# Order in the first attention of an adaptive block: queries scaled by ScalarE, transposes ahead of maxima, gathers behind divisions, merges ahead of the last product

## The chip, the cores and the metric

The kernel runs on one core of a Trainium2 chip. Its engines are named as in the profile: PE (TensorE, matmuls; PEld is its loading of weights), DVE (VectorE), ACT (ScalarE), POOL (GpSimd) and SP (SyncE, which issues most of the transfers). The metric is the time on the device in microseconds (us), as a median of several runs. The time before is 1429.85 us (three runs, 1428.89 to 1431.21).

## The reference

The block computes, on `x` of 8 batches of 128 tokens by 512 values:

```python
x = x + attn(cond(x, weight, adapter_ids), wq, wk, wv, wo)
x = x + ffn(cond2(x, ...))

def cond(x, weight, adapter_ids):          # a 512x512 matrix per batch
    return jnp.einsum('bsi,boi->bso', x, weight[adapter_ids])

def attn(x, wq, wk, wv, wo):               # 32 heads of 16, 8 pairs of keys and values
    q = (x @ wq).reshape(b, s, 32, 16)
    k = jnp.repeat((x @ wk).reshape(b, s, 8, 16), 4, axis=2)
    v = jnp.repeat((x @ wv).reshape(b, s, 8, 16), 4, axis=2)
    scores = jnp.einsum('bihd,bjhd->bhij', q, k) * 16 ** -0.5
    scores = jnp.where(causal, scores, finfo.min)
    out = jnp.einsum('bhij,bjhd->bihd', softmax(scores), v)
    return out.reshape(b, s, 512) @ wo
...
```

`cond2` is a second attention, with 32 heads of 128, rotary positions, and a cache of keys and values of which pages are looked up in a table. `ffn` is a matrix product with low-rank matrices added, one pair chosen for each batch and one shared. All numbers are float32.

## The kernel before

The kernel has two parts that share the core one after the other: the first attention (with the conditioning matrix), up to about 224 us, and the second attention with the feed-forward, which takes the rest. Both are written as explicit sequences: a manual schedule keeps every engine's instructions in the order in which the Python code issues them. The framework adds the semaphores: an instruction waits until what it reads is written and until the buffer that it writes is free, and what stands behind it on the same engine waits too.

The first attention is a loop over `k` from 0 to 16 (L719). Each batch `b` has two steps, an even one (`hb == 0`, k = 2b) and an odd one (k = 2b + 1), and each step handles half of the batch's heads. Within a step the probabilities lie in two tiles, `n` = 0 and 1.

- `scores1(k)` (L586): TensorE writes the causal mask (L595) and adds the products of scaled queries and keys (L607) in two PSUM tiles of 128x1024. At its end VectorE takes the negated row maxima of both tiles (L616).
- `exps1(k, n)` (L628): ScalarE, eight exponentials for each tile (L635), which read the scores and the maxima.
- `divide1(k, n)` (L639): VectorE sums and inverts (L643, L644), then GpSimd multiplies the 128x1024 tile by the inverses (L645).
- `turn1(k)` (L649): VectorE transposes both tiles of a step in blocks of 32x32 (L655). It is issued for the step before, `last`, directly behind the scores and maxima of the step at hand.
- `values1(b, groups)` (L659): TensorE multiplies the transposed probabilities by the values (L671), and VectorE copies the result (`oT`, L683). It is issued in the even step for the batch before, in two halves.
- `condition(b)` (L507): TensorE multiplies the transposed input by the gathered matrix (`hp`, L514), and VectorE copies it out (`hT`, L522; by ScalarE for batch 0). In the even step, for the next batch; then its keys (`project_k`, L545) and values (`project_v`, L552) are projected from `hT`.
- `project_q(b, ...)` (L530) and `keep_q(b)` (L538): in the odd step, the queries of the next batch, 16 matmuls (32 rows of the trace), and VectorE's scaling of the 128x512 tile into `qT` (L540). Behind it `flip_x` (L502) transposes a later batch's input, which ScalarE copies (L505).
- `out_proj1(b)` (L690): in the odd step, the output product (L693), the residual addition by VectorE (L697) and a store. `flip_x1` (L700) transposes the sum in the next even step, with a copy by ScalarE (L702).
- `gather_w(b)` (L293): GpSimd issues four indirect transfers (L296) of the conditioning matrix of a batch. It is called at the end of the even step, for batch b + 3.
- `indices()` (L374): VectorE works out the addresses for the cached pages (L377 to L382), in the odd step of batch 0. They are first read by `gather(0, ...)`, in the odd step of batch 6. `tables(0)` and `tables(1)` are GpSimd work (L414 to L416) in the odd steps of batches 1 and 2.
- `merge_gates` (L441, L447, VectorE, at the end of step 12), `merge_a` (L457, step 14), `merge_b` (L469) and `merge_w` (L484) prepare the low-rank matrices of the feed-forward. `merge_b(h)` is eight rows of TensorE in the trace, a copy by ScalarE (L477) and a store; `merge_w(i)` two, with an addition by VectorE (L491).

In the last step (k = 16) only the values product of batch 7 is left. Before it, in step 15, the first unit of the second attention is projected (`q_matmul`, `q_turn`, `kv_matmul`, `kv_turn`, `norms`). Step 16 issues, in this order: both transposes, `flip_x1(6)`, `queries(0)` (transposes of the first unit's queries, L254), the first half of `values1(7)`, `merge_b(0)`, its second half, `merge_b(1)`, `merge_w(0)` and `merge_w(1)`. Behind the loop come `keys(0)` (L263), `own_keys(0)` (L271) and the other two `merge_w`.

PSUM tiles that matter: `p_mm` (tag `mm`, two buffers) holds the projections, the output product and the merges; `p_tp` (two buffers) the flips and the values product; `p_sc` (two buffers) the scores.

Of the kernel before, what the change touches and what calls it, by code (L numbers as in the profile page):

```python
# [14 lines left out]
AF = mybir.ActivationFunctionType  # L15
ALU = mybir.AluOpType
# [4 lines left out]
B, S, DM = 8, 128, 512  # L21
# [8 lines left out]
SCALE1 = HD1 ** -0.5  # L30
# [11 lines left out]
def block_kernel(  # L42
# [28 lines left out]
    nc = tc.nc  # L71
# [178 lines left out]
    def queries(u):  # L250
        s = st[u]
        tp = p_tp.tile([P, REP, S], F32, tag="tp", name=f"qTp_{u}")
        for r in range(REP):
            nc.tensor.transpose(tp[:, r, :], s["qa"][:, r, :], ident[:])  # L254
        s["qT"] = tile_a([P, REP, S], f"qT_{u}")
        nc.scalar.copy(s["qT"][:], tp[:])  # L256
# [19 lines left out]
    with (  # L276
# [216 lines left out]
        xT, hT, qT, kbd = {}, {}, {}, {}  # L493
# [43 lines left out]

        def keep_q(b, ps):  # L538
            qT[b] = p1.tile([P, REP, S], F32, tag="qT1", name=f"qT1_{b}")
            nc.vector.tensor_scalar(qT[b][:], ps[:], SCALE1, None, ALU.mult)  # L540

        def project_k(b):
            ps = p_mm.tile([P, 2, P], F32, tag="mm", name=f"kvp1_{b}")
# [40 lines left out]
        H = [{} for _ in range(2 * B)]  # L584

        def scores1(k):  # L586
            b, hb = divmod(k, 2)
            h = H[k]
            h["sc"] = [
                p_sc.tile([P, 2, 4 * S], F32, tag="sc", name=f"sc1_{k}_{n}") for n in range(2)  # L590
            ]
            for c in range(4):
                for j in range(4):
                    rows = slice(32 * j, 32 * j + 32)
                    nc.tensor.matmul(  # L595
                        h["sc"][j // 2][:, j % 2, :].rearrange("p (n t) -> p n t", n=4)[
                            :, :, 32 * c : 32 * c + 32
                        ],
                        causal[rows, c, :],
                        eye32[rows],  # L600
                        start=(c == 0),
                        stop=False,
                    )
            for rr in range(2):
                for j in range(4):
                    rows = slice(32 * j, 32 * j + 32)
                    nc.tensor.matmul(  # L607
                        h["sc"][j // 2][:, j % 2, rr * 2 * S : (rr + 1) * 2 * S],
                        qT[b][rows, 2 * hb + rr, :],
                        kbd[b][rows].rearrange("p h t -> p (h t)"),  # L610
                        start=False,
                        stop=(rr == 1),
                    )
            h["nm"] = p1.tile([P, 2, 8], F32, tag="nm1", name=f"nm1_{k}")
            for n in range(2):
                nc.vector.tensor_reduce(  # L616
                    h["nm"][:, n, :],
                    h["sc"][n][:].rearrange("p j (h t) -> p (j h) t", t=S),
                    AX.X,
                    ALU.max,  # L620
                    negate=True,
                )
# [3 lines left out]
        prs = {}  # L626
# [19 lines left out]
                pr, pr, sums[:].unsqueeze(2).to_broadcast([P, 8, S]), ALU.mult  # L646
            )

        def turn1(k):  # L649


            b, hb = divmod(k, 2)
            for n in range(2):
                pr = prs[b, n][:, hb].rearrange("p m t -> p (m t)")
                nc.vector.transpose(pr, pr)  # L655

        oT = {}

# [55 lines left out]
        ps = new_q(0)  # L714
# [4 lines left out]
        for k in range(2 * B + 1):  # L719
            b, hb = divmod(k, 2)  # L720
            more, now, last = b + 1 < B, k < 2 * B, k - 1
            if now:
                scores1(k)
            if k:
                turn1(last)
            if hb == 0:
                if b >= 2:
                    flip_x1(b - 2)
                if now:
                    exps1(k, 0)  # L730
                if more:
                    condition(b + 1)
                if k == 2 * B - 2:
                    for i in range(KC):
                        merge_a(i)
                if now:
                    exps1(k, 1)
                if k == 2 * B:
                    queries(0)
                if k:  # L740
                    values1(b - 1, (1, 0))
                if now:
                    divide1(k, 0)
                if more:
                    kv = project_k(b + 1)
                if k == 2 * B:
                    merge_b(0)
                if k:
                    values1(b - 1, (3, 2))
                if now:  # L750
                    divide1(k, 1)
                if more:
                    project_v(b + 1, kv)
                    keep_k(b + 1, kv)
                if k == 2 * B:
                    merge_b(1)
                    for i in range(2):
                        merge_w(i)
                if more:
                    keep_v(b + 1, kv)  # L760
                gather_w(b + 3)
                if k == 2 * B - 4:
                    merge_gates()
            else:
                if b >= 1:
                    out_proj1(b - 1)
                exps1(k, 0)
                exps1(k, 1)
                divide1(k, 0)
                divide1(k, 1)  # L770
                if more:
                    ps = new_q(b + 1)
                    project_q(b + 1, ps, range(REP - 1))
                else:
                    for c in range(KC):
                        q_matmul(0, c)
                    for part in q_turn(0):
                        part()
                    for c in range(KC):
                        kv_matmul(0, c)  # L780
                if more:
                    project_q(b + 1, ps, (REP - 1,))
                    keep_q(b + 1, ps)
                else:
                    kv_turn(0)
                    norms(0)
                if b + 2 < B:
                    flip_x(b + 2)
                load_x(b + 4)
                if b == 0:  # L790
                    indices()
                elif b == 1:
                    tables(0)
                    load_qkv(0)
                    load_wo(0)
                elif b == 2:
                    tables(1)
                    nc.gpsimd.memset(minus_half[:], -0.5)
                elif b == 3:
                    load_qkv(1)  # L800
                elif b == B - 2:
                    gather(0, "kg")
                    gather(0, "vg")
                if b == 4:
                    nc.sync.dma_start(out=bias[:], in_=ffn_b.unsqueeze(0).to_broadcast([P, DM]))
                    merge_loads()
# [257 lines left out]
    for u in range(N + 1):  # L1064


        now, nxt, last = u < N, u + 1 < N, 1 <= u <= N
# [146 lines left out]
```

## Time and profile before

| | us |
|---|---|
| median of three runs | 1429.85 (1428.89 to 1431.21) |
| the profiled execution | 1425.54 |
| its span, first to last instruction | 1423.8 |
| first attention, up to the first L901 | 224.6 |
| TensorE busy from 224 to 1424 us | 1189 of 1200 |

How TensorE fares in the first attention, by pairs of steps (the last two rows are the end of the loop and what stands behind it):

| stretch, us | TensorE busy | granted clock |
|---|---|---|
| 24 to 47 | 19.0 of 23 | 0.93 |
| 47 to 68 | 19.8 of 21 | 1.00 |
| 68 to 89 | 20.2 of 21 | 1.00 |
| 113 to 134 | 20.2 of 21 | 1.00 |
| 155 to 176 | 17.2 of 21 | 0.89 |
| 176 to 200 | 22.1 of 24 | 0.95 |
| 200 to 224 | 19.7 of 24 | 0.76 |

A line of the timeline gives the start, the time from the first to the last of a group of equal instructions, the engine, the line of the kernel, the operation, out<-in with shapes, how many, and in brackets how long the engine had been idle and what ended that. A line of the waits gives who waited for whom, then the total, how often, and the longest. A line of the stages gives the stretch, the busy time and number of instructions of TensorE, its weight loads, VectorE, ScalarE and GpSimd, then the granted clock of TensorE as a share of full speed, and the share and rate of the transfers.

### The profile page before, as it was taken

How to read it: one execution, taken by the hardware profiler on the slowest of the kernel's cores; microseconds unless marked ns; L12 is line 12 of the kernel's file. 1: busy time of each engine (PE TensorE's matmuls, PEld its weight loads, DVE VectorE, ACT ScalarE, POOL GpSimd, SP SyncE). 2: the span in 40 equal slices, each digit the busy share in tenths (PEclk: the TensorE clock that was granted, in tenths of full speed). 3: DMA queues.
4: the chain of work that ended last, by engine and by line, in shares of the span. 5: the costliest groups of instructions: out<-in, count | busy, mean ns of one | idle time of the engine just before them, and what ended most of it. 6: DMA issues, size and time to landing. Idle time of an engine off the chain costs nothing.

```text
span 1423.8 us, 21814 instructions
## 1 busy us (share of the span) xinstructions
PE 1383.9 (97%) x7012; PEld 893.8 (63%) x7012; DVE 945.2 (66%) x2274; ACT 641.3 (45%) x1496; POOL 567.8 (40%) x553
## 2 busy tenths in 40 slices
PE   7899889999999999999999999999999999999998
PEld 6777655666666666666666666666666565666555
DVE  5877854666666666666666666666666665666651
ACT  3444424444444444444444444444444444344431
POOL 6675342433333333333333333333333333343220
PEclk9999989999999999999999999999999999999999
DMA  6354412544444565444445654444456544434430
GB/s 220 109 165 153 149 35 66 162 119 118 118 119 116 159 189 155 119 120 118 120 119 159 191 153 119 118 118 121 119 158 191 153 120 136 129 109 114 117 111 30
DMA packets 161968, 185.60 MB, mean 130 GB/s; under 512 B 93056, under 2 KB 103552, under 8 KB 161856
## 3 DMA queue, kind: packets, MB, share of 16 engines
q1 hardware_dynamic: 146304, 139.64, 35.0%
q0 software_dynamic: 15552, 44.58, 10.7%
q8 instruction: 56, 0.92, 0.3%
q14 instruction: 56, 0.46, 0.1%
HBM read 80.03 MB, written 5.77 MB: 60 GB/s over the span
## 4 chain that ended last, share of the span: by engine, by line
PE 87%; DVE 8%; issue 2%; POOL 1%; DMA 1%; SPq 1%; ACT 0%; DVEq 0%; POOLq 0%
PE op L975 19%; PE sc L901 15%; PE qp L177 15%; PE yp L994 15%; PE kvp L217 7%; PE sc L908 4%; DVE pr L655 2%; DVE nm L616 2%; PE fp L1056 2%; PE qTp L254 2%; PE o L671 2%; DVE sums L643 1%; PE sc L607 1%; PE beff L469 1%; PE kvp L545 1%
## 5 line engine op out<-in xcount | busy, mean ns | idle before, releaser
L914 DVE CUSTOM_DVE_ANT_0 pr<-sc,mask,nq 128x640 f32<-128x640 f32 x256 | 226.0, 884 | 143.3 <-PE sc L908 131.4
L924 ACT ACTIVATE pr<-pr,nm 128x640 f32<-128x640 f32 x256 | 211.9, 828 | 189.4 <-DVE nm L914 186.3
L901 PE MATMUL sc<-kT,qT 128*128 128x512 f32 x512 | 263.9, 598 | 0.0
L177 PE MATMUL qp<-wq,x1T 128*128 128x512 f32 x512 | 251.5, 594 | 0.0
L975 PE MATMUL op<-pT,vg 128*128 128x256 f32 x1024 | 242.1, 380 | 1.3 <-DMA pT<-fl 1.3
L203 POOL TENSOR_TENSOR qa<-qa,qb 128x512 f32<-128x512 f32 x64 | 81.6, 1276 | 379.7 <-DVE sums L891 379.7
L994 PE MATMUL yp<-wo,oT 128*128 128x512 f32 x504 | 227.5, 594 | 0.0
L975 PEld LDWEIGHTS op<-pT,vg 128*128 128x128 f32 x1024 | 194.4, 191 | 27.1 <-DVE sums L891 1.6
L892 ACT ACTIVATE pr<-pr,sums 128x640 f32<-128x640 f32 x256 | 208.4, 814 | 0.0
L895 DVE STREAM_TRANSPOSE fl<-pr 128x640 f32<-128x640 f32 x252 | 189.2, 808 | 0.0
L908 PEld LDWEIGHTS sc<-kTo,qT 128*128 128x128 f32 x512 | 97.2, 191 | 125.3 <-issue 103.9
L994 PEld LDWEIGHTS yp<-wo,oT 128*128 128x128 f32 x504 | 91.0, 191 | 91.6 <-issue 90.2
L160 POOL DMA_INDIRECT kg<-in_k_cache_dram,idx_kv x128 | 132.0, 1031 | 35.3 <-issue 34.9
L160 POOL DMA_INDIRECT vg<-in_v_cache_dram,idx_kv x128 | 128.1, 1001 | 37.8 <-issue 33.0
L901 PEld LDWEIGHTS sc<-kT,qT 128*128 128x128 f32 x512 | 88.3, 192 | 80.9 <-issue 78.8
L256 ACT COPY qT<-qTp 128x512 f32<-128x512 f32 x64 | 37.5, 585 | 210.6 <-PE qTp L254 207.3
L217 PEld LDWEIGHTS kvp<-wkv,x1T 128*128 128x128 f32 x512 | 97.5, 190 | 40.3 <-issue 30.3
L217 PE MATMUL kvp<-wkv,x1T 128*128 128x256 f32 x512 | 121.0, 380 | 0.0
L244 POOL TENSOR_TENSOR rs<-ss,minus_half 128x5 f32<-128x5 f32 x64 | 76.4, 1194 | 83.0 <-DVE ss L242 82.1
L177 PEld LDWEIGHTS qp<-wq,x1T 128*128 128x128 f32 x512 | 83.2, 192 | 32.0 <-issue 32.0
L908 PE MATMUL sc<-kTo,qT 128*128 128x128 f32 x512 | 99.8, 277 | 0.0
L273 ACT COPY kTo<-kTp 128x128 f32<-128x128 f32 x64 | 17.0, 266 | 162.5 <-PE kTp L271 162.5
(152 smaller groups left out, 1676.3 us busy)
## 6 DMA issues: line engine op xcount, KB each, us to landing
pT<-fl SPq DMA_DIRECT2D x1008, 80.0 KB
kT<-flk SPq DMA_DIRECT2D x480, 32.0 KB
wq<-in_wq_dram SPq DMA_DIRECT2D x8, 1024.0 KB
wo<-in_wo_dram SPq DMA_DIRECT2D x8, 1024.0 KB
vrep<-v_kept SPq DMA_DIRECT2D x32, 128.0 KB
wkv<-in_wkv_dram SPq DMA_DIRECT2D x8, 512.0 KB
kg<-in_k_cache_dram,idx_kv POOLq DMA_INDIRECT x128, 3.6
vg<-in_v_cache_dram,idx_kv POOLq DMA_INDIRECT x128, 3.5
```

The source lines that it names most:

```text
L160: nc.gpsimd.indirect_dma_start(out=dst[:, c].rearrange("p n d -> p (n d)"), out_offset=None, in_=src, in_offset=bass.IndirectOffsetOnAxis( ...
L177: nc.tensor.matmul(s["qp"][:].rearrange("p h d -> p (h d)"), x1T[b][:, c, :], weights[g][0][:, c, :], start=(c == 0), stop=(c == KC - 1),)
L203: nc.gpsimd.tensor_tensor(qa[:], qa[:], qb[:], ALU.add)
L217: nc.tensor.matmul(s["kp"][:], x1T[b][:, c, :], weights[g][1][:, c, :], start=(c == 0), stop=(c == KC - 1))
L892: nc.scalar.activation(prs[r][:], prs[r][:], AF.Copy, scale=sums[:, r : r + 1])
L895: nc.vector.transpose(s["flips"][:, :, :, r, :].rearrange("p b c j -> p c b j"), prs[r][:])
L901: nc.tensor.matmul(sc[:, : NBLK * P].rearrange("p (k j) -> p k j", j=32), s["qT"][:, r, :], s["kT"], start=True, stop=True,)
L908: nc.tensor.matmul(sc[:, NBLK * P : NK], s["qT"][:, r, :], s["kTo"][:], start=True, stop=True)
L914: nc.vector.tensor_tensor_reduce(out=pr[:], in0=sc[:, :NK], in1=mask[:], scale=s["nq"][:, r : r + 1], scalar=3.0e38, op0=ALU.add, op1=ALU.min,
L924: nc.scalar.activation(pr[:], pr[:], AF.Exp, bias=nm[:, r : r + 1], scale=-1.0, accum_out=sums[:, r : r + 1],)
L975: nc.tensor.matmul(ops[h][:, : 2 * S], cached(u, "vg", c) if c < NBLK else s["vo"][:], s["pT"][:, :, c, 2 * h : 2 * h + 2, :].rearrange("p ...
L994: nc.tensor.matmul(yp[:], s["oT"][:, r, :], weights[g][2][:, r, :], start=(r == 0), stop=(r == REP - 1))
```

## The change

Six things are edited, all in the first attention:

- `keep_q` scales with ScalarE (`activation` with Copy and a scale) in place of VectorE.
- The maxima become a function of their own, `max1`, and `turn1` handles one tile. In even steps both transposes of the step before are issued ahead of the maxima. In odd steps the maxima come first, then the transpose of tile 0; that of tile 1 is issued behind the divisions.
- `gather_w(b + 3)` moves from the end of the even step to the odd step, behind the divisions.
- `indices()` moves from the odd step of batch 0 to that of batch 5.
- In step 16 both `merge_b` are issued ahead of `queries(0)`.
- In step 16 `merge_w(0)` and `merge_w(1)` are issued between the two halves of `values1(7)`.

No instruction is added or removed but the eight scalings, which change engine.

```diff
         def keep_q(b, ps):
             qT[b] = p1.tile([P, REP, S], F32, tag="qT1", name=f"qT1_{b}")
-            nc.vector.tensor_scalar(qT[b][:], ps[:], SCALE1, None, ALU.mult)
+            nc.scalar.activation(qT[b][:], ps[:], AF.Copy, scale=SCALE1)
...
+        def max1(k):
+            h = H[k]
             h["nm"] = p1.tile([P, 2, 8], F32, tag="nm1", name=f"nm1_{k}")
             for n in range(2):
                 nc.vector.tensor_reduce(
...
-        def turn1(k):
+        def turn1(k, n):
             b, hb = divmod(k, 2)
-            for n in range(2):
-                pr = prs[b, n][:, hb].rearrange("p m t -> p (m t)")
-                nc.vector.transpose(pr, pr)
+            pr = prs[b, n][:, hb].rearrange("p m t -> p (m t)")
+            nc.vector.transpose(pr, pr)
...
             if now:
                 scores1(k)
-            if k:
-                turn1(last)
             if hb == 0:
+                if k:
+                    turn1(last, 0)
+                    turn1(last, 1)
+                if now:
+                    max1(k)
                 if b >= 2:
                     flip_x1(b - 2)
...
                 if k == 2 * B:
+                    merge_b(0)
+                    merge_b(1)
                     queries(0)
                 if k:
                     values1(b - 1, (1, 0))
...
                 if k == 2 * B:
-                    merge_b(0)
+                    for i in range(2):
+                        merge_w(i)
                 if k:
                     values1(b - 1, (3, 2))
...
-                if k == 2 * B:
-                    merge_b(1)
-                    for i in range(2):
-                        merge_w(i)
                 if more:
                     keep_v(b + 1, kv)
-                gather_w(b + 3)
                 if k == 2 * B - 4:
                     merge_gates()
             else:
+                max1(k)
+                turn1(last, 0)
                 if b >= 1:
                     out_proj1(b - 1)
                 exps1(k, 0)
                 exps1(k, 1)
                 divide1(k, 0)
                 divide1(k, 1)
+                turn1(last, 1)
+                gather_w(b + 3)
...
-                if b == 0:
+                if b == 5:
                     indices()
```

## The prediction

> **What bounds the kernel now.** I read the page first, for the busy shares and the chain that ended last.
>
> ```profile
> PE 1383.9 (97%) x7012; PEld 893.8 (63%) x7012; DVE 945.2 (66%) x2274; ACT 641.3 (45%) x1496; POOL 567.8 (40%) x553
> ...
> PE 87%; DVE 8%; issue 2%; POOL 1%; DMA 1%; SPq 1%; ACT 0%; DVEq 0%; POOLq 0%
> ```
>
> TensorE is the bound, and the chain leaves it mostly for VectorE. Cut into stages, TensorE is busy 1189 of the 1200 us after 224 us, where the second attention begins (its first scores, L901, start at 224.63). The change edits only what lies before. So a microsecond of TensorE idle time or of slow clock saved there should reach the end whole. Next I read the waits of the first 230 us (total, times, longest):
>
> ```profile
> PE sc L607 <- DVE qT L540: 5.7, 7, 2.6
> ...
> PE o L671 <- DVE pr L655: 2.0, 7, 0.6
> ...
> PE sc L607 <- DVE iota_sf L377: 2.0, 1, 2.0
> ```
>
> The scores wait for scaled queries and the last product for transposes. The timeline of one even step (k=10; start, duration) shows how:
>
> ```profile
> 127.02 3.75 POOL L645 TENSOR_TENSOR pr<-pr,sums 128x1024 f32<-128x1024 f32 x2 [0.26 <-DVE sums L644]
> ...
> 127.98 0.58 ACT L505 COPY xT<-xTp 128x512 f32<-128x512 f32 x1 [2.19 <-PE xTp L499]
> ...
> 128.11 0.64 DVE L540 TENSOR_SCALAR qT<-qp 128x512 f32<-128x512 f32 x1
> ...
> 128.80 1.15 PE L607 MATMUL sc<-kbd,qT 32*128 32x256 f32 x16 [0.57 <-DVE qT L540]
> ...
> 129.98 2.35 DVE L616 TENSOR_REDUCE nm<-sc 128x8 f32<-128x1024 f32 x2 [1.23 <-PE sc L607]
> ...
> 132.26 2.36 DVE L655 STREAM_TRANSPOSE pr<-pr 128x1024 f32<-128x1024 f32 x2
> ...
> 134.54 0.65 DVE L522 COPY hT<-hp 128x512 f32<-128x512 f32 x1
> 134.67 1.07 PE L671 MATMUL o<-pr,vrep 32*32 32x128 f32 x40 [0.21 <-DVE pr L655]
> ```
>
> The query product ends at 127.45, but VectorE reaches it at 128.11, behind two sums; ScalarE sits idle 2.19 us there. Per pair of steps (20.86 us) TensorE loses only 0.57 + 0.21 = 0.78 us. More is lost in the last step (k=16):
>
> ```profile
> 199.02 0.60 ACT L204 ACTIVATE sq<-qp 128x512 f32<-128x512 f32 x1 [3.81 <-PE x1Tp L499]
> ...
> 201.46 0.66 PE L254 MATMUL qTp<-ident,qa 128*128 128x128 f32 x4 [3.01 <-POOL qa L203]
> ...
> 204.63 0.77 PE L671 MATMUL o<-pr,vrep 32*32 32x128 f32 x8 [2.52 <-issue]
> ...
> 207.57 6.14 PE L469 MATMUL beff<-lb,gs 128*128 128x512 f32 x8
> ...
> 215.58 3.70 PE L469 MATMUL beff<-lb,gs 128*128 128x512 f32 x8
> ```
>
> Two idle gaps, and then the same eight matmuls take 6.14 us once and 3.70 once. The stages' granted clock (before the last two columns) says why:
>
> ```profile
> 208.00:211.00 3.00, 3.00 (x4) 1.08 (x4) 0.17 (x1) 0.00 (x0) 0.00 (x0) 0.50 0.02 5
> ...
> 223.00:226.00 3.00, 3.00 (x4) 0.96 (x4) 1.85 (x4) 0.00 (x0) 0.00 (x0) 0.50 0.02 4
> ```
>
> In slices of 1 us the clock is half from 202.4 to 212.7, and from 222.9 to 229.7.
>
> **Part by part.** Times are those of the old trace unless said.
>
> 1. Queries on ScalarE. Eight VectorE scalings (0.64) become eight ScalarE activations on the same 128x512 PSUM tile; the nearest row is L505, 0.58. ScalarE's exponentials (L635) end at 125.8, so it starts at about 127.54 and ends at 128.13, when the mask matmuls (L595) end at 128.23. The wait goes: 0.57 in k=4, 6, 10, 12 and 0.32 in k=8: 2.6 us. The flip copy L505, now behind it, ends near 128.7; its product starts at 130.4. In k=0 ScalarE is free at 22.5 and the product ends at 22.76; the table load (1.28, at 22.54) then follows and ends by 24.8, ahead of the exponentials at 26.06: nothing changes.
>
> 2. Transposes. In the odd step one transpose (1.2) moves behind the divisions, so the residual add (L697) follows the out product at 144.85, not 145.71. Sums and divisions move up: old start 147.87, now 147.01, end 150.76. T(k-1, second) runs 148.1-149.3, T0 to 150.4, T1 waits for the second division and ends at 152.05; behind it in VectorE's queue stand the maxima, for which the exponentials wait, ending at 154.35, and hT, at 155.0. The key product L545, next on TensorE, now arrives at 155.7 (156.52 less 0.78). So hT has 0.6 us to spare, and the last product finds its transposes ready: 0.21 in five steps, 1.05 us. The maxima are late by 1.2 us against old; exponentials follow and end near 157.5; the next scores need those PSUM buffers at 159.9. If that cover went, each microsecond beyond it would be paid in each pair.
>
> 3. Gathers. Four at about 1.25 us leave GpSimd before the odd divisions and stand behind them: 150.8 to 155.8, with the next division due at 157.9. They land half a pair later, for a product a pair and a half away: nothing. At b=1 and b=2 the tables (6.45 us, L414 to L416) now push the even divisions to about 76 and 97; their transposes, behind the odd maxima, are due at 77.8 and about 97.4 to 101.8, so 0, at worst 1.
>
> 4. Indices leave step 1 for step 11. In step 2, the maxima waited for them until 43.54, and the product ran at a clock of 0.64 (5.47 us for 3.74). Now scores can start at 38.9 (exponentials end 38.17, scaling 0.59) for 40.58. The VectorE chain then sets the end: sums to 39.55, divisions to 41.7, transposes to 43.2, maxima to 45.55, hT to 46.2, L545 at 46.3 for 49.22: gain 2.9 (1.5 if the clock still falls). In step 11, the indices (0.14, 2.62, 0.35) stand ahead of T0. The 2.62 us row ended at 43.24, as two divisions of GpSimd (39.44 to 43.20) did; idx_w, the same kind with 8 columns for 32, took 0.23. Nearer the stretched reading: they end when the divisions do, T0 starts at 151.15 and L545 is 0.85 us late. Bounds: 0 (short) and 2.2 (2.62 intrinsic). I take 0.85.
> The Trainium skill, "SBUF — State Buffer", section "SBUF: two separate sides", says VectorE and GpSimd share a port pair that one of them holds for a whole instruction. The row agrees; by the rule the cost would again be about 0.85.
>
> 5. Step 14. Gates (L447) still hold the maxima of step 13 to 164.79, and exponentials end at 170.26. Scaling on ScalarE lets scores start at 171.0, for 173.28. The four merge_a products then start at 172.8, but the third needs a PSUM buffer that VectorE empties behind the maxima (175.55 to 177.9), so it starts at 178.4 and the fourth ends at 181.9 for 184.36: 2.4; 1.4 if the clock is half there, as before. I take 2.0.
>
> 6. Last step. With those 2.0 off, the x1 flip ends at 196.45. Both merge_b products, now first, need the buffers of the first projections: VectorE reads to 197.2, the square (0.60) to 197.9. Then 2 x 3.70 to 205.3, query flip 0.6, values 1.5 (their transposes end at 204.0, ahead), two merge_w 2.0, values 2.0 to 211.4, wait for oT 0.4, key flips 0.9, merge_w 2.0: the first scores at 214.6 for 224.63. That is 10.0, of which 8.0 is new; their 5.0 us at half clock (224.63 to 229.66) cost 2.5 more, which could go. The clock changes come 10.3, 10.2 and 6.8 us apart, multiples of 3.4; one such stretch at half loses 1.7. I charge two: one after the 1.5 us gap at 196.4 (a gap of 1.5 us at 94.0, releaser "issue", was followed by a clock of 0.52 in 97 to 100), one after merge_w and flips, which filled TensorE from 219.4 to 222.9 and were followed by half clock. 8.0 + 2.5 - 3.4 = 7.1; bounds 10.5 and 2.5.
> The Trainium skill, "TensorE: Matmul & The Clock Gate", "HAM oscillation", asks only that gaps stay under some 3.4 us. By it the first charge falls and the sum would be 1.7 larger; the gap at 94 differs, and I keep the charge.
>
> Sum: 2.6 + 1.05 + 2.9 - 0.85 + 2.0 + 7.1 = 14.8 us. The profiled execution took 1425.54 (span 1423.8), so 1410.7; it lies 4.3 under the median 1429.85, so 1415 is the forecast for the median.
>
> **Rivals.** A, slow clock at the end: query flip, values, merge_w and key flips now stand together, and if all of it runs at half (values 2.7 as at 204.6, merge_w 2.88 as at 221.8, the other values 3.6, flips 1.7, wait 0.4), first scores come at 220.1 and the step is worth 2.5: total 10.2, 1419.6. For: the drop at 222.9. Against: 185 to 190, mostly values, kept 1.00.
> B, VectorE becomes the bound of a pair: 0.8 us more in the handoffs of point 2 use up the margin, and 3.65 goes: 1418.7. For: the margin is 0.6. Against: all durations are measured.
> C, slower: VectorE's transposes and maxima can't run while GpSimd writes the gathers' descriptors. Place: 150.8 to 155.8 in the five pairs with gathers. Price: up to 5.0 - 0.6 = 4.4 each, 22 in all, so 1437; it turns the sign from 14.8 / 5 + 0.6 = 3.6 us late per step. For: the stretched row of point 4. Against: transposes at 122.57 beside gathers took 2.36, as elsewhere.
> That the edits do not reach the engines is out: in the built order each engine has them as written.
>
> **Chances.** Forecast (1411 to 1418) 0.60; A 0.17; B 0.10; C 0.08; better (no slow window, 1411.6 or less) 0.05. Range 1410 to 1423: it takes in A and B and the bounds of points 4 to 6. Faster by over 0.2% (under 1427; 0.2% is about what a measurement of this kernel can tell from nothing) 0.87, same 0.05, slower 0.08.
>
> **What would show it.** No wait of L607 for queries; the pair at 20.1 us; L545 right behind the last product except in steps 2 and 12; merge_b twice at 3.7 to 5.4; first L901 near 211 (224.6 less the gains up to there, 15.7, with one slow stretch). Wrong if L545 waits for hT in every pair, if the gathers' rows stretch the transposes, or if the second attention grows.

## The result, and the profile after

| | before | after |
|---|---|---|
| median of six runs each, us | 1429.59 (1425.64 to 1433.33) | 1441.11 (1438.57 to 1443.13) |
| profiled span, us | 1423.8 | 1436.8 |
| first scores of the second attention (L901 before, L909 after), us | 224.63 | 236.72 |
| from there to the end, us | 1199.1 | 1200.1 |

The changed kernel is slower: ratio 1.008, 95% interval 1.006 to 1.0099. The forecast was 1415.0 us in a range of 1410 to 1423, faster. The second attention hardly moved, so 12.1 of the 13.0 us between the profiled spans were lost ahead of it. Of these, 1.2 lie ahead of the first scores of step 0 (24.82 for 23.63), a start that lies between 23.5 and 26.2 in the runs below; 10.9 were lost in the loop.

First the page of the changed kernel: busy time by engine, the granted clock in 40 slices of the span, and the shares of the chain that ended last.

```profile
PE 1398.5 (97%) x7012; PEld 903.6 (63%) x7012; DVE 940.0 (65%) x2266; ACT 645.5 (45%) x1504; POOL 568.5 (40%) x553
...
PEclk9898998999999999999999999999999999999999
...
PE 90%; DVE 4%; issue 2%; SPq 1%; DMA 1%; POOL 1%; ACT 1%; another core or an unknown queue 0%; DVEq 0%; POOLq 0%; ACTq 0%
```

TensorE has the same 7012 instructions and is busy 14.6 us longer (1383.9 before): the same work ran slower. The clock is under 0.9 in the second, fourth and seventh slice, all within the first 252 us (a 9 stands for 0.9 or more). Now TensorE's waits in the first 240 us of the changed kernel (total, times, longest):

```profile
PE o L673 <- issue: 5.5, 9, 1.0
...
PE sc L607 <- ACT qT L540: 1.5, 1, 1.5
```

The waits for scaled queries shrank as meant, from 5.7 us in seven to 1.5 in one. In their place stands a line without a partner: TensorE sat in the values product (L673) for 5.5 us in nine gaps of up to 1.0 us, and "issue" means that the profile names nothing that was being waited for. Before, that product had two such gaps, 4.0 us in all, one of them the 2.52 us in the last step.

The table gives the distance from the scores (L607) of one step to those of another; the last row runs to the first scores of the second attention. The third column is the experiment that puts only the gathers back, told below. Each column is one profiled execution; the old order of steps 0 to 14 takes 149.65 us in this one and 147.60 in another (that of e7 below), so some 2 us of a sum can be chance.

| steps | before | after | gathers back |
|---|---|---|---|
| 0 to 4 | 39.58 | 41.56 | 41.77 |
| 4 to 6 | 20.85 | 21.50 | 19.66 |
| 6 to 8 | 23.89 | 24.59 | 20.65 |
| 8 to 10 | 20.85 | 26.30 | 19.65 |
| 10 to 12 | 20.86 | 24.73 | 19.89 |
| 12 to 14 | 23.62 | 21.55 | 21.55 |
| 14 to 15 | 14.85 | 18.34 | 15.11 |
| 15 to the end | 36.50 | 33.33 | 31.66 |
| sum | 201.00 | 211.90 | 189.94 |

Against the third column the loss is in the pairs whose product now runs beside gathers of the matrix (k = 4 to 10) and in step 14, whose product runs beside the cache gathers that step 13 always issued. Steps 0 to 4 lose as much with the gathers back, but for another reason (point 4 below). From step 12 to 14, where no gather of the matrix is left, the changed kernel is faster.

One such place in the changed kernel's timeline, the first half of the values product of k = 10 (48 rows):

```profile
143.13 0.95 POOL L296 DMA_INDIRECT cw<-in_cond_w_dram,idx_w  x1 [0.30 <-issue]
144.00 0.65 PE L673 MATMUL o<-pr,vrep 32*32 32x128 f32 x29
...
144.39 0.94 POOL L296 DMA_INDIRECT cw<-in_cond_w_dram,idx_w  x1 [0.30 <-issue]
...
144.86 0.41 PE L673 MATMUL o<-pr,vrep 32*32 32x128 f32 x4 [0.21 <-issue]
144.89 0.69 DVE L522 COPY hT<-hp 128x512 f32<-128x512 f32 x1 [0.94 <-PE hp L514]
...
146.31 0.70 PE L673 MATMUL o<-pr,vrep 32*32 32x128 f32 x15 [1.03 <-issue]
```

The transposes are ready, so 29 rows go through without a pause. Then TensorE stops, does four rows, stops for 1.03 us, and goes on 0.98 us after GpSimd's last gather ended at 145.33. In k = 4, 6, 8 and 10 the stops come after 28 to 37 rows, and the 48 rows take 2.94, 2.92, 3.02 and 3.01 us; without gathers they take 1.10 (k = 12). That is 1.8 to 1.9 us each. Most of the rest goes with the clock. The stages of the changed kernel around that stop (the columns as before; the granted clock stands ahead of the last two):

```profile
145.00:148.00 3.00, 1.97 (x27) 1.43 (x25) 1.54 (x4) 2.16 (x9) 0.33 (x1) 1.00 1.02 222
148.00:151.00 3.00, 3.00 (x106) 2.98 (x109) 0.86 (x2) 0.00 (x0) 1.90 (x1) 0.52 1.04 334
```

Behind the stop the clock is half for 6.83 us (148.09 to 154.92). It is half for 6.83 us behind that of k = 6 (96.89 to 103.72) and for 10.24 behind that of k = 8 (120.79 to 131.03); only k = 4 keeps full speed. The pairs of the changed kernel, and behind them the same pairs of the one with the gathers back, by stages:

```profile
87.90:112.50 24.60, 23.45 (x325) 18.78 (x324) 16.88 (x23) 11.00 (x40) 17.86 (x15) 0.86 0.57 184
112.50:138.80 26.30, 25.28 (x324) 19.96 (x324) 16.86 (x23) 10.99 (x40) 11.42 (x9) 0.81 0.32 100
138.80:163.50 24.70, 23.46 (x320) 18.87 (x321) 16.83 (x23) 10.96 (x40) 11.35 (x9) 0.86 0.80 264
```

```profile
86.90:107.60 20.70, 19.84 (x327) 15.95 (x322) 16.93 (x23) 11.03 (x40) 18.54 (x16) 1.00 0.70 232
107.60:127.20 19.60, 19.60 (x324) 15.93 (x320) 16.81 (x23) 10.94 (x40) 10.68 (x8) 1.00 0.38 117
127.20:147.10 19.90, 19.73 (x327) 15.93 (x320) 16.93 (x23) 11.01 (x40) 8.22 (x6) 1.00 0.71 222
```

The same 320 to 327 rows of TensorE take 23.5 to 25.3 us at a clock of 0.81 to 0.86, and 19.6 to 19.8 at 1.00. VectorE's time is the same.

### The profile page after: what moved, and what is told of

Its sections match the earlier page's. It is cut to its first block, busy times and chain, and to the rows that moved or that the text cites. A ratio compares the mean times of both kernels' runs of the same rounds, so it can differ in the third digit from the quotient of the medians.

```text
span 1436.8 us, 21822 instructions
## 1 busy us (share of the span) xinstructions
PE 1398.5 (97%) x7012; PEld 903.6 (63%) x7012; DVE 940.0 (65%) x2266; ACT 645.5 (45%) x1504; POOL 568.5 (40%) x553
## 4 chain that ended last, share of the span: by engine, by line
PE 90%; DVE 4%; issue 2%; SPq 1%; DMA 1%; POOL 1%; ACT 1%; another core or an unknown queue 0%; DVEq 0%; POOLq 0%; ACTq 0%
PE op L983 18%; PE qp L177 15%; PE sc L909 15%; PE yp L1002 14%; PE kvp L217 7%; PE sc L916 4%; PE o L673 2%; PE fp L1064 2%; PE qTp L254 2%; PE att L695 2%; PE hp L514 1%; PE qp L530 1%; SPq L956 1%; PE sc L607 1%; PE kvp L552 1%
## 5 line engine op out<-in xcount | busy, mean ns | idle before, releaser
L909 PE MATMUL sc<-kT,qT 128*128 128x512 f32 x512 | 263.5, 596 | 0.0
L909 PEld LDWEIGHTS sc<-kT,qT 128*128 128x128 f32 x512 | 88.2, 192 | 80.9 <-issue 78.7
L648 POOL TENSOR_TENSOR pr<-pr,sums 128x1024 f32<-128x1024 f32 x32 | 60.4, 1898 | 84.5 <-DVE sums L647 72.9
```

What stands on the lines that cost most here:

```text
L909: nc.tensor.matmul(sc[:, : NBLK * P].rearrange("p (k j) -> p k j", j=32), s["qT"][:, r, :], s["kT"], start=True, stop=True,)
```

## The experiments

Each time stands beside that of the old kernel on the same chip, and is read as a ratio with its 95% interval. The theory from these rows: the gathers, now issued beside the values product, stop TensorE there, and the stops take the clock down. Rivals: the whole order is slower; or it is the megabyte that the gathers move, not their issue.

### 1. Gathers back, and gathers alone

`e1_gathers_back`, against the changed kernel:

```diff
                 if more:
                     keep_v(b + 1, kv)
+                gather_w(b + 3)
...
                 turn1(last, 1)
-                gather_w(b + 3)
```

> The changed kernel with gather_w back at the end of the even step; all other edits stay. In the changed kernel TensorE stood idle about 1 us, with no releaser named, inside the values product of k=4, 6, 8, 10 and 14, each time while GpSimd wrote gathers or just behind, and in k=6, 8, 10 its clock was half afterwards for 6.8 to 10.2 us. Theory 'collision' (gathers beside the values product stop TensorE): those idle times go and the kernel takes 1412 to 1422. Rival 'chain' (transposes ahead of the maxima make VectorE the bound of a pair): nothing changes, 1437 to 1444.

Measured 1417.11 us (1414.31 to 1418.86), old kernel 1427.08: ratio 0.993 (0.9909 to 0.995). No gap of the values product is put down to "issue" any more, and the clock is full from 59.4 to 206.1. One moved call turns a loss of 0.8% into a gain of 0.7%: some 21 us (0.015 of 1429; 22.0 by the table's sums).

`e2_gathers_alone`, against the old kernel:

```diff
-                gather_w(b + 3)
...
                 divide1(k, 1)
+                gather_w(b + 3)
```

> The kernel before with one edit: gather_w behind the odd step's divisions. Theory 'collision': idle times of about 1 us without releaser appear in the values product, the clock falls behind some, 8 to 20 us slower than before (1438 to 1450). Rival 'chain': the transposes' order is that of before, so 1427 to 1433.

Measured 1430.56 (1427.29 to 1433.03), old 1427.08: 1.0029 (1.0014 to 1.0044). The loss is there, but is 4 us and not the 11 or more expected. The first halves of the product run beside gathers here too (k = 4: product 71.10 to 72.80, gathers 70.52 to 72.71) and do not stop; they still pause after eight rows for a transpose. Long gaps without a releaser come, up to step 14, only in the second halves: 0.95 us in k = 6, where the old kernel has one of 1.48 at the same row with no gather near, and 1.98 in k = 10, which is new; no half clock follows. They are of another kind, told in the last section. The scores of k = 6 also wait 1.88 us for queries, with GpSimd's tables pushed later. So gathers beside the product are not enough by themselves: the move cost a few microseconds on the old order and 21 on the new one.

### 2. Traffic or issue

`e3_plain_copy` adds to the old kernel, behind the odd divisions, a plain copy of 1 MB that SyncE issues, behind a small memset and store that time it; `e4_tiny_gathers` adds there four indirect transfers of GpSimd with rows of 16 bytes:

```diff
+        def extra(b):
+            if b + 3 < B:
+                t = p1w.tile([P, KC, 4], F32, tag="extra", name=f"extra_{b}")
+                for c in range(KC):
+                    nc.gpsimd.indirect_dma_start(out=t[:, c, :], out_offset=None,
+                        in_=cond_w.rearrange("r (a d) -> (r a) d", d=4),
+                        in_offset=bass.IndirectOffsetOnAxis(ap=idx_w[:, c, b : b + 1], axis=0))
...
                 divide1(k, 1)
+                extra(b)
```

> The kernel before, its gathers untouched, and in batches 0 to 4 a memset of GpSimd behind the odd divisions, for which SyncE waits and then issues a copy of 1 MB in rows of 2 KB from one tensor in DRAM to another: the volume of one batch's gathers, at the time where the change puts them, without GpSimd's work. Theory 'traffic' (the transfers themselves hold up TensorE): idle times in the values product and 6 to 20 us slower than before. Theory 'descriptors' (GpSimd's writing of the gathers does it): within 3 us of before.

> The kernel before, its gathers untouched, and in batches 0 to 4 four more indirect transfers behind the odd divisions, of 16 bytes in a row for 2 KB, so that GpSimd writes as many descriptors as the gathers need and hardly anything moves. Theory 'descriptors': idle times in the values product and 6 to 20 us slower. Theory 'traffic': within 3 us of before.

Measured, against 1427.08: the copy 1428.05 (1.0002, 0.9982 to 1.0021), the tiny gathers 1432.82 (1.0044, 1.0027 to 1.0061). But neither has a new stop: the one of e4 (1.65 us in k = 6) is the old kernel's, and its loss comes with a wait of 1.88 us for queries behind a fuller GpSimd. Since the old order has no stop beside gathers to begin with, both were repeated on the kernel of e1, `e5_tiny_beside_e1` with `extra` behind `turn1(last, 1)`, `e6_copy_beside_e1` with the copy there.

> The changed kernel with the gathers put back behind the even step (which ran at 1417.1 us), and with four more indirect transfers of 16-byte rows behind each odd division of batches 0 to 4; what they fetch is not used. If it is the making of an indirect transfer that stops TensorE, the stops are back in the first half of the values product (about 1 us in k = 4, 6, 8, 10) with half-clock stretches behind them, and the time is 1430 to 1445. If it is the 1 MB of traffic that the gathers move, these 64 KB leave it at 1414 to 1421.

> The same base (1417.1 us) with a plain 1 MB copy inside the device's memory, in rows of 2 KB, issued by SyncE at the time of the odd divisions of batches 0 to 4; what it copies is not used. Traffic as the cause: stops back, 1430 to 1445. Making of the indirect transfers as the cause: no stops, 1414 to 1421.

Measured, against 1431.72: the tiny gathers 1446.24 (1.0102, 1.0076 to 1.0127), the copy 1424.79 (0.9961, 0.9937 to 0.9985). The timeline of e5, k = 8:

```profile
123.05 0.65 PE L673 MATMUL o<-pr,vrep 32*32 32x128 f32 x27
123.42 0.95 POOL L710 DMA_INDIRECT extra<-in_cond_w_dram,idx_w  x1 [0.30 <-issue]
...
123.97 0.30 PE L673 MATMUL o<-pr,vrep 32*32 32x128 f32 x2 [0.28 <-issue]
...
125.41 0.73 PE L673 MATMUL o<-pr,vrep 32*32 32x128 f32 x19 [1.14 <-issue]
...
125.45 0.69 DVE L522 COPY hT<-hp 128x512 f32<-128x512 f32 x1 [2.45 <-remote]
```

Transfers of 2 KB each (128 rows of 16 bytes, 40 KB in all, not the 64 KB that the expectation says) give the changed kernel's picture: 27 rows, a stop, and TensorE on again 1.04 us after the last of them ended at 124.37. The stops are in k = 4, 6, 8 and 10, each with half clock behind it (6.8 to 10.2 us). So it is not the amount of data. In e6 SyncE got to the copy late in three steps (in k = 8 at 114.60, when the first half had run from 112.70 to 113.80), but in k = 4 it came in time. First e6, with its stage (the last number is GB/s), then the stage of e5's stop in k = 4:

```profile
71.59 0.51 SPq L713 DMA_DIRECT2D copy<-in_cond_w_dram  x1
71.77 1.10 PE L673 MATMUL o<-pr,vrep 32*32 32x128 f32 x48
```

```profile
71.77:72.87 1.10, 1.10 (x50) 0.90 (x49) 0.69 (x1) 1.10 (x6) 1.10 (x2) 1.00 0.84 265
```

```profile
71.77:74.81 3.04, 1.77 (x49) 0.97 (x48) 0.69 (x1) 3.04 (x13) 2.72 (x4) 1.00 0.21 60
```

The 48 rows took 1.10 us beside 265 GB/s, and 3.04 us beside 60 GB/s and indirect transfers. e6 has no stop in k = 4 to 12, but four in k = 14 (2.3 us in all), beside the cache gathers, and half clock there, which e1 has not. No copy is near (the last was issued at 138.14), and e7 below stops there without any.

### 3. Indirect transfers, or any that GpSimd issues

`e10_plain_by_gpsimd` replaces e5's four indirect transfers by plain ones of the same size. They ended 1.40 us ahead of the product in k = 4, 0.65 in k = 10 and 0.09 in k = 8, and reached 0.12 us into it in k = 6, so `e13_nine_plain` issues nine:

```diff
-                    nc.gpsimd.indirect_dma_start(...)
+                    nc.gpsimd.dma_start(out=t[:, c, :], in_=cond_w[c * P : (c + 1) * P, :4])
...
-                t = p1w.tile([P, KC, 4], ...)
-                for c in range(KC):
+                t = p1w.tile([P, 9, 4], ...)
+                for c in range(9):
```

> The kernel of e5_tiny_beside_e1 (1446.2 us) with its extra indirect transfers replaced by plain ones of the same size, also issued by GpSimd; what they fetch is not used. If any transfer that GpSimd issues stops TensorE's run of small matmuls, the stops stay: 1430 to 1447. If only indirect ones do, there are none: 1414 to 1421.

> The kernel of e10_plain_by_gpsimd with nine plain transfers of 16-byte rows by GpSimd in place of four, which at 0.56 us each last as long as the four indirect ones (5.0 us) and reach into the values product; what they fetch is not used. If any transfer that GpSimd issues beside the product stops TensorE, the stops of about 1 us are back in k = 4 to 10 and the time is 1430 to 1447. If only the indirect kind does, there are none: 1416 to 1424.

Measured: four, 1419.83 against 1426.55 (0.9962, 0.9942 to 0.9982); nine, 1422.73 against 1426.95 (0.998, 0.9962 to 0.9998). The timeline of e13, first k = 6, then k = 10:

```profile
93.41 1.25 DVE L657 STREAM_TRANSPOSE pr<-pr 128x1024 f32<-128x1024 f32 x1 [0.60 <-POOL pr L648]
...
94.71 1.07 PE L673 MATMUL o<-pr,vrep 32*32 32x128 f32 x40 [1.26 <-DVE pr L657]
...
97.55 2.07 PE L545 MATMUL kvp<-hT,wk_sb 128*128 128x128 f32 x8 [1.77 <-DVE hT L522]
...
137.90 4.33 POOL L710 DMA_DIRECT2D extra<-in_cond_w_dram  x8
...
140.78 1.10 PE L673 MATMUL o<-pr,vrep 32*32 32x128 f32 x48
```

In k = 10 the plain transfers are being issued through the whole first half, and its 48 rows take 1.10 us; so it is in k = 4 and 8. In these first halves only the indirect kind stopped TensorE. The one gap, in k = 6, is an ordinary wait: GpSimd's longer queue (the tables and the nine transfers) made a division and so a transpose late. It shows one thing more: 1.26 us of waiting in the same small matmuls and 1.77 us behind them, for hT, both ordinary waits with no gather beside them, were followed by half clock from 97.51 to 107.75. So the clock can fall behind waits alone. Which of the two did it is not shown, nor that every such gap does it (in k = 4 of the changed kernel none followed).

### 4. Overlap, or number

`e14_two_and_two`, against the changed kernel, leaves two of the four gathers behind the odd divisions and issues the other two at the old place:

```diff
                     keep_v(b + 1, kv)
+                gather_w(b + 3, (0, 1))
...
                 turn1(last, 1)
-                gather_w(b + 3)
+                gather_w(b + 3, (2, 3))
```

> The changed kernel with two of the four gathers of a batch behind the odd divisions and the other two at their old place. The two end some 2.5 us sooner, ahead of the values product. If it is the overlap of their issue with the product that stops TensorE, the stops are gone and the time is that of all gathers back: 1414 to 1421. If gathers in the odd step cost by their number, half of the 24 us stays: about 1429.

Measured 1414.86 (1410.60 to 1416.44) against 1426.95: 0.9917 (0.9889 to 0.9944). Its timeline at k = 10 (lines are one higher):

```profile
125.08 0.99 POOL L297 DMA_INDIRECT cw<-in_cond_w_dram,idx_w  x1
126.37 0.95 POOL L297 DMA_INDIRECT cw<-in_cond_w_dram,idx_w  x1 [0.30 <-issue]
...
128.49 1.10 PE L674 MATMUL o<-pr,vrep 32*32 32x128 f32 x48
128.60 0.69 DVE L523 COPY hT<-hp 128x512 f32<-128x512 f32 x1
```

The gathers end at 127.32, 1.17 us ahead of the product, and nothing stops. Half of the moved gathers stayed, and none of the loss. It is the time at which they are issued. (Its steps 0 to 4 take 36.02 us for e1's 41.77, with only two gathers ahead of step 2's divisions; see 6.)

### 5. The prediction's other steps, one by one

`e7_merges_alone` makes only the two moves of the last step in the old kernel, `e8_queries_alone` only the scaling on ScalarE:

```diff
-            nc.vector.tensor_scalar(qT[b][:], ps[:], SCALE1, None, ALU.mult)
+            nc.scalar.activation(qT[b][:], ps[:], AF.Copy, scale=SCALE1)
```

> The old kernel with the two moves of the last step alone (both merge_b ahead of the queries, merge_w between the halves of the product). The prediction's step 6 says 7.1 us less than the old kernel (2.5 to 10.5): 1417 to 1425, first scores of the second attention at about 217.5. If the last step only trades one half-clock stretch for another, it is within 2 us of the old kernel's 1428 and the first scores start at 222 or later.

> The old kernel with the query scaling on ScalarE alone. The prediction's steps 1, and of step 5 what the early queries bring: 2.6 plus up to 2.0 us, so 1423 to 1427 for an old kernel at 1428, with no wait of the scores for queries in k = 4 to 12. If the waits only move to the product's transposes (the maxima, begun earlier, hold nothing back, but the divisions are no sooner), it is 1427 to 1429 and the wait of the values product for transposes grows from 0.21 to about 0.8 in each even step.

Measured, against 1431.72: merges 1426.72 (0.9962, 0.9949 to 0.9976), 5.0 us by the medians; from the scores of step 15 on, 31.8 us for 36.5. Its first scores of the second attention start at 223.32 all the same, and not near 217.5: steps 14 to 15, which e7 does not edit, took 18.72 us for 14.85. Queries 1434.29 (1.0026, 1.001 to 1.0041), slower, where both theories had it faster or equal. Its profile shows where: from the scores of step 0 to those of step 14 it takes 144.97 us, for 149.65 in the old kernel's profile and 147.60 in e7's, which has the old code there; so 2.6 to 4.7 were gained. Then comes step 14, of e8 and behind it of e7:

```profile
180.03 0.86 PE L671 MATMUL o<-pr,vrep 32*32 32x128 f32 x38
...
180.53 0.95 POOL L160 DMA_INDIRECT vg<-in_v_cache_dram,idx_kv  x1 [0.30 <-issue]
181.31 0.42 PE L671 MATMUL o<-pr,vrep 32*32 32x128 f32 x4 [0.41 <-issue]
...
182.74 0.42 PE L671 MATMUL o<-pr,vrep 32*32 32x128 f32 x4 [1.00 <-issue]
...
186.21 1.08 PE L671 MATMUL o<-pr,vrep 32*32 32x128 f32 x25 [1.75 <-DVE oT L683]
```

```profile
183.01 0.86 PE L671 MATMUL o<-pr,vrep 32*32 32x128 f32 x30
...
184.89 0.41 PE L671 MATMUL o<-pr,vrep 32*32 32x128 f32 x4 [0.47 <-issue]
186.32 0.65 PE L671 MATMUL o<-pr,vrep 32*32 32x128 f32 x13 [1.02 <-issue]
```

The product of step 14 runs beside the cache gathers that step 13 has always issued, and here it stopped. From there to step 15 e8 takes 20.72 us for 14.85, with half clock from 184.4 to 194.7. So a gain upstream was given back by the same collision at a place that nobody had edited. That the gain brought the stop on is not shown: e7 stopped there without one, and the old kernel's half (184.29 to 185.38) ran through beside a gather issued from 184.16 to 185.10.

### 6. Step 2 and the last step

Two half-clock stretches are left in e1: 49.1 to 59.4 and 206.1 to 219.8. On e1's kernel, `e9_maxima_first_k2` takes the maxima ahead of the transposes in step 2 alone; `e11_merge_between` puts merge_b(1) between the halves of the last product and merge_w behind them; `e12_both` does both.

```diff
+                if k == 2:
+                    max1(k)
                 if k:
                     turn1(last, 0)
                     turn1(last, 1)
-                if now:
+                if now and k != 2:
                     max1(k)
...
                     merge_b(0)
-                    merge_b(1)
                     queries(0)
...
-                    for i in range(2):
-                        merge_w(i)
+                    merge_b(1)
                 if k:
                     values1(b - 1, (3, 2))
+                if k == 2 * B:
+                    for i in range(2):
+                        merge_w(i)
```

> The changed kernel with the gathers put back (1417.1 us), and in step 2 alone the maxima ahead of the transposes, as in the old order. In step 2 the gathers hold the divisions to 45.1, and so in the new order the transposes, the maxima behind them and hT. If that, and the 1.77 us gap of the key product that ends in half clock (49.1 to 59.4), is what ate the gain that step 4 of the prediction saw in step 2, the key product starts some 2 us sooner, the scores of step 3 at 52 to 55 for 57.25, and the time is 1412 to 1415. If the clock falls anyway, it is 1415 to 1417.

> The changed kernel with the gathers put back (1417.1 us), and in the last step the order merge_b(0), queries, first half of the product, merge_b(1), second half, merge_w. If it is the stretch of small matmuls and waits in a row (202.0 to 206.1) that takes the clock to half (206.1 to 219.8), full-array products between them keep it, the first scores of the second attention come 3 to 6 us sooner, and the time is 1411 to 1414. If the clock falls at the loop's end whatever the order, it is 1416 to 1421.

> Both edits, of e9_maxima_first_k2 and e11_merge_between, on the changed kernel with the gathers put back (1417.1 us). If both half-clock stretches go, 1406 to 1411; if neither does, 1415 to 1420.

Measured, against 1426.55: e9 1413.03 (0.9911, 0.9882 to 0.994), e11 1416.68 (0.9929, 0.9894 to 0.9963), e12 1414.62 (0.9924, 0.9899 to 0.995). Step 2 in e1:

```profile
41.32 3.76 POOL L648 TENSOR_TENSOR pr<-pr,sums 128x1024 f32<-128x1024 f32 x2
...
45.11 1.25 DVE L657 STREAM_TRANSPOSE pr<-pr 128x1024 f32<-128x1024 f32 x1 [0.60 <-POOL pr L648]
...
46.28 2.32 DVE L619 TENSOR_REDUCE nm<-sc 128x8 f32<-128x1024 f32 x2
...
49.25 2.08 PE L545 MATMUL kvp<-hT,wk_sb 128*128 128x128 f32 x8 [1.77 <-DVE hT L522]
```

GpSimd comes out of batch 3's gathers at 41.3, the second transpose waits for its division until 45.11, the maxima and hT queue behind, and TensorE stands for 1.77 us; the clock is half from 49.1. In e9 the maxima no longer stand behind the division, the key product (1.16 us) follows the values at once, the clock stays full, and steps 0 to 4 take 36.10 us for e1's 41.77. Of the last step, e11's profile shows 29.7 us for e1's 31.7 and half clock for 6.8 us in place of 13.7, but the times of the two kernels cover the same range, so nothing is settled there; e12 is no better than e9. e9, e12 and e14 all beat both kernels and are not told apart from one another, nor by their intervals from e1.

## Why the prediction was wrong, point by point

**The step that failed is point 3**, "for a product a pair and a half away: nothing", with "0, at worst 1". It followed the gathers down GpSimd's queue and to their landing, and asked only who waits for either. It never asked what runs on TensorE while they are issued, although its own figures put the gathers at 150.8 to 155.8 and the key product, which follows the first half of the values, at 155.7. At the old place that was the output and query products; at the new one it is 48 rows of the smallest matmuls of the kernel, which stop. The table prices it: the columns "after" and "gathers back" differ by 1.84, 3.94, 6.65 and 4.84 us in the four pairs, 3.23 in step 14 and 1.67 behind step 15, less 0.21 ahead of step 4: 22.0 us (21 by the measured ratios). Of this the longer products are 9.2 (1.84 + 1.82 + 1.92 + 1.91 + 1.68); the other 12.8 goes with 30.7 us of half clock that e1 does not have there (6.83 + 10.24 + 6.83 in the pairs, 3.41 + 3.41 in steps 14 and 15), worth up to 15.4. The part of steps 14 and 15, 4.9 of the 22.0, is the least certain: the cache gathers there were not moved, and the same code stops there in one profile (e7) and not in another.

**Point 2 laid the trap.** It was right that the transposes would be ready, and undersized: the pause is 0.21 us, but the first half takes 1.10 us without it for 1.70 with it. With the queries' 0.57 that makes 1.17, and the pair 8 to 10 fell by 1.20 with the gathers back, for 0.78 predicted. But in e2, with the pause, the first halves never stopped beside gathers, and in the changed kernel, without it, they stopped in four pairs. The two parts were priced one by one and the price lies in the pair. That the pause itself protects is an inference from these two kernels, and from e4 and e5, which differ in the same way; it was not tried alone.

**Points 1 and 5 were right in kind.** 2.6 and 2.0 us were forecast up to step 14; e8 shows 4.68 against the old kernel's profile and 2.63 against e7's, so the size is settled to within 2 us only. What e8 then lost in step 14 was not foreseen.

**Point 4 was right up to the key product and lost what came behind it.** Step 2 of the changed kernel:

```profile
44.76 1.48 PE L673 MATMUL o<-pr,vrep 32*32 32x128 f32 x48
...
46.86 0.95 POOL L296 DMA_INDIRECT cw<-in_cond_w_dram,idx_w  x1 [0.31 <-issue]
...
47.12 1.16 PE L545 MATMUL kvp<-hT,wk_sb 128*128 128x128 f32 x8 [0.89 <-DVE hT L522]
48.92 0.49 DVE L685 COPY oT<-o 128x128 f32<-128x128 f32 x2 [1.86 <-remote]
...
49.27 3.85 PE L673 MATMUL o<-pr,vrep 32*32 32x128 f32 x112 [0.99 <-DVE oT L685]
```

The key product (L545) starts 22.30 us after the scores of step 0, for 25.59 before: 3.3 us gained, where 2.9 were forecast. But VectorE copied oT only at 48.92, 1.1 us after the last gather ended, though what it copies was done at 46.24 and it had stood idle 1.86 us ("remote": the profile names no engine). The second half waited 0.99 us for it, the clock was half from 49.1 to 59.3, and steps 0 to 4 took 2.0 us more than before. It is the picture of the stops beside gathers, here on VectorE; no run isolates it. With the gathers back the same steps lose 2.2 us for another reason: the divisions stand behind gathers, to 45.08, and the new order puts the maxima behind the divisions. e9 undoes that one handoff and gains 3.5. In step 12 the indices cost about what was forecast: with the gathers back, their long row (L378) again ends with the divisions (148.83 and 148.79), and the key product waits 0.93 us for hT, where 0.85 were forecast.

**Point 6 had the mechanism and overstated the size:** 4.8 us with the gathers back and 4.7 in e7 (15 to the first scores of the second attention), for 7.1, of which its "near 211" puts 6.3 ahead of those scores; inside the bounds. Two half-clock stretches of 3.4 us were charged, and with the gathers back there were four (13.65 us from 206.13). All edits but the gathers' move together gave 10.0 us (1427.08 to 1417.11) of the 14.8 forecast.

**Rival C** named the right place, sign and nearly the sum ("22 in all, so 1437"), with the wrong mechanism. VectorE's transposes take 1.22 us at the median from 60 to 163 us in the old kernel and 1.20 in the changed one, and at most 1.25 beside gathers; TensorE is what stops, and VectorE stands idle ahead of single rows (the last section). Its chance of 0.08 rested on VectorE's rows alone.

**The clock.** In the changed kernel, gaps of 1.0 to 1.2 us in all among small matmuls were followed by half clock in three pairs of four, in e5 in four of four, and in e13 two ordinary waits of 1.26 and 1.77 us were. It is no rule: in k = 4 of the changed kernel, and behind e2's gap of 1.98 us, the clock stayed full. The Trainium skill, "TensorE: Matmul & The Clock Gate", section "HAM oscillation", worries about gaps of more than some 3.4 us; these rows differ from it, and its next section, "A second HAM failure mode: psum-queue depth-cycling", which tells of short and frequent idling between groups of matmuls, is nearer to what was seen. The prediction kept a charge for such gaps at the end of the loop, and did not think of one inside the pairs.

## What to carry to other kernels

When a transfer's issue is moved, look at what every engine runs in the new place, not only at who waits for the queue and the data: in this order indirect transfers stopped nothing beside large products and cost 22 us beside a run of tiny ones, and 1.2 us of distance was enough to be rid of it. A stop of a microsecond among small matmuls should be priced with the half clock that may follow it, which here was worth as much as the stop or more (12.8 us went with it, 9.2 with the longer products). And price edits in pairs where one removes the wait that kept another harmless; a gain can be given back at a place that nobody touched (step 14 of e8), so read from the steps where it went before the edit is judged.

## What the runs showed of the hardware that was not expected

- Indirect transfers issued by GpSimd, 2 KB or 256 KB each, stopped TensorE in runs of 32x32 matmuls for about 1 us without any wait in the profile; plain transfers by GpSimd, nine in 4.9 us beside the same rows, did not. In k = 4 to 10 TensorE went on 0.90 to 0.98 us after the end of the last gather in the changed kernel, and 1.00 to 1.04 us after it in e5, however long it had stood. In all eight the product started 0.81 to 0.88 us after the start of the last gather but one; in step 2 of the changed kernel it started 0.41 us after that of one with two more behind it, and the 48 rows took 1.48 us without a gap of over 0.15.
- VectorE seems to be held as well. It stood idle without a named engine for 1.86 us in step 2 of the changed kernel, ahead of oT, and for 1.94 to 2.45 us in k = 2, 4, 6 and 8 of e5, ahead of oT or hT; each time it went on 1.0 to 1.2 us after the end of the last gather. The old kernel, e1 and e14 have no such row up to 200 us. The 0.80 to 0.86 us by which hT starts late in k = 4, 8 and 10 of the changed kernel (0.04 in e14) prove less: ahead of hT VectorE is idle for 1.06 us in k = 6 and 10 of e1 too, without gathers.
- Not every overlap stops. In step 14 of e1 the first half (179.53 to 180.62) ran at full rate with a cache gather issued from 179.67 to 180.61; in e6, nearly the same alignment (179.68; 179.83 to 180.77) stopped four times. What inside the chip holds TensorE, and what tells these cases apart, is open.
- There is a second kind of gap without a releaser, and it fits a shortage of instructions. The 1.48 us in the second half of k = 6 of the old kernel ended 1.37 us after the end of a 16 KB instruction transfer, 0.54 us in e7 1.33 after one, e2's 0.95 and 1.98 us 1.48 and 1.55 after one, and 2.29 us in e14, ahead of L553, 1.52 after one. The stops beside gathers do not fit it: in k = 4 to 10 of the changed kernel and of e5 the last such transfer had ended 4.4 us or more before the stop's end (for the stop of k = 4 in the changed kernel, 72.86 to 73.87, the nearest start at 68.15 and 77.03). That the second kind waits for instructions is an inference from these times.
- GpSimd needs 0.54 us to issue a plain transfer of 128 rows and 1.25 us for an indirect one, the gap behind it included.
